# Two degree sums of A moved from the fifth strip of an attention to the first, and the last row block loaded at its 20 rows

## The chip, the cores and the metric

The kernel runs on one core of one Trainium2 chip. The metric is the device time of one execution in microseconds (us). The time before is the median of three runs, 733.3 us (730.9 to 733.57).

## The reference

The graph has 2708 nodes with 128 features and a dense 0/1 adjacency matrix A in float32. Layer 0 needs, among other things, the degree of each node (the row sums of A), and an attention over neighbours; layer 1 is left out here except for its last line, since the change does not touch it.

```python
deg = jnp.clip(adj.sum(axis=1), 1.0)
dis = deg ** (-0.5)
adj_norm = dis[:, None] * adj * dis[None, :]
diffusion = adj_norm @ x - x
norms = jnp.maximum(jnp.linalg.norm(x, axis=-1), COS_EPS)
sim = x @ x.T / (norms[:, None] * norms[None, :])
attn = jax.nn.softmax(beta * sim * adj, axis=1)
...
return diffusion + jax.nn.sigmoid(alpha) * (attn @ x - x)
...
x = _layernorm(x + _L0_gnn_ref(L0_gnn_t, x, adj, L0_gnn_alpha, L0_gnn_beta), axis=-1)
x = _layernorm(x + _L1_gnn_ref(x, adj, L1_gnn_W, L1_gnn_a), axis=-1)
```

## The kernel before

The nodes are cut into NB = 22 blocks of P = 128 (the last, block 21, has LAST = 20 valid nodes) and into NS = 6 strips of SW = 512 columns (the last has 148). A and its transpose are both in HBM; they are padded with zero rows to 22 full blocks.

**The attention** (lines 496 to 641) goes over the strips in the order 2, 3, 4, 0, 1, 5. The position in this order is n, from 0 to 5: "the first strip" is n = 0, "the fifth" is n = 4, and the narrow strip of 148 columns comes last, n = 5. Within a strip it goes over all 22 blocks, and k counts them from 0 to 21. For each k, TensorE makes the similarities `sim` in a PSUM bank (a matmul from the normalized rows `xn_t`, lines 560 to 563; or, where the same block pair has been computed in an earlier strip, four transposes of what was kept in `turned`, lines 553 to 558). VectorE multiplies them by `gentle` and by a piece of A (`piece`) into `p_t` (line 565), ScalarE takes the exponential in place (`grown`, line 591), GpSimd adds it to `total` (line 594), and TensorE accumulates `att_acc` from it (`weighed`, line 603). The buffers are four PSUM banks for `sim`, six for `p_t` and five for `piece`.

**The degrees** ride along in the attention. `degree(ib, h)` (line 456) loads one half row block of A, 128 x 1354 (677 KB), into one of two `row` buffers through SyncE's queue, and ScalarE copies it in place with a running sum into `deg2[:, ib, h]`. The 44 half rows stand in `todo` in the order of the blocks; the table `rows_at` (line 519) says at which k of which strip the next one is taken. `roots(b0, b1)` (line 465) turns the sums of a stretch of blocks into `dis`: three small operations on VectorE (writing `deg`, `live`, `deg`) and one power on GpSimd. It is called for blocks 0 to 7 at n = 2, for 8 to 17 at n = 4, k = 5, and for 18 to 21 at n = 4, k = 19 (line 514).

In the first strip two more things lie on ScalarE: the normalized rows are copied from PSUM to `xn_t` after they have been transposed (`turn_rows`, line 365). At k = 17 this is done for blocks 4 to 7, which are taken from k = 18 on (line 527).

**The last strip** (n = 5) also scales `x_sb` by `dis` in place (line 636), in five operations on VectorE over 6, 6, 5, 3 and 2 blocks. They have to wait until the attention's matmuls have read the rows they overwrite.

**The diffusion** follows (lines 776 to 782 and 865 on): for each strip, 22 matmuls with the scaled `x_sb` and a strip of the transpose (`strip`), which `load_strip` (line 765) loads in two halves of 11 blocks, 2.8 MB each, through SyncE's queue. Strips 0, 1 and 5 are loaded ahead of the diffusion. GpSimd issues loads of `nat`, 768 KB each, on its own queue (line 693); the first four stand right behind its last `total`.

**What sets the order.** Each engine runs its instructions in one order fixed when the program is built. A scheduler places them by priority and by a cost model; instructions made through `pinned` keep the order in which they were written on their engine. The whole first strip up to k = 20 is pinned on all engines (`strict`), `degree` pins its ScalarE copy everywhere, and `in_order` pins what it wraps. SyncE issues loads in its own order too, and waits there for the buffer of each.

Of the kernel before, what the change touches and what calls it, by code (L numbers as in the profile page):

```python
# [10 lines left out]
AF = mybir.ActivationFunctionType  # L11
# [4 lines left out]
P = 128  # L16
N = 2708
D = 128
NB = (N + P - 1) // P
# [26 lines left out]
def grouped(  # L46
# [14 lines left out]
    nc = tc.nc  # L61
# [10 lines left out]
    def width(s):  # L72
        return min(SW, N - s * SW)
# [86 lines left out]
    deg2 = const.tile([P, NB, 2], F32, name="deg2")  # L160
# [11 lines left out]
    def pinned(engine, op, *args, **kwargs):  # L172
        with ExitStack() as e:
            if engine in latest:
                e.enter_context(tc.issue_after(latest[engine].ins))
            latest[engine] = op(*args, **kwargs)  # L176
            return latest[engine]
# [31 lines left out]
    def to_sbuf(acc, v, nb):  # L209

        t = lp.tile([P, SW], F32, tag="to_rows", name="tr_sb", bufs=2)
        if v < nb * P:
            nc.gpsimd.memset(t[:, v : nb * P], 0.0)
        act("copy", t[:, :v], acc[:, :v])
        return t

    def turned(t, nb, ps):

        rows = ps.tile([P, SW // P, P], F32, tag="tp", name="tr_ps")
        for b in range(nb):  # L220
            mm(nc.tensor.transpose, rows[:, b, :], t[:, ts(b, P)], ident)
        return rows
# [76 lines left out]
    with ExitStack() as es:  # L299
# [156 lines left out]
        def degree(ib, h):  # L456

            z = pa.tile([P, N // 2], F32, tag="row", name="row", bufs=2)
            nc.sync.dma_start(z, adj[ts(ib, P), h * (N // 2) : (h + 1) * (N // 2)])
            pinned(  # L460
                "ACT", nc.scalar.activation, z, z, AF.Copy,
                accum_out=deg2[:, ib, h : h + 1],
            )

        def roots(b0, b1):
# [25 lines left out]


        todo = [(ib, h) for ib in range(NB) for h in range(2)]
        ended = None
        scaled = set()
        for n, s in enumerate(order):
# [4 lines left out]
            if v < nb * P:  # L501
# [15 lines left out]
            }  # L517

            rows_at = {
                0: (18, 20), 1: range(0, NB, 2), 2: range(0, NB, 2), 3: range(0, NB, 2),  # L520
                4: range(0, 18, 2), 5: (),
            }
            turns = {
                3: lambda: turn_rows(12, 16, by_dve),
# [20 lines left out]
            for k, jb in enumerate(blocks_j):  # L545
# [77 lines left out]
                if k in rows_at[n]:  # L623
                    in_order(lambda: degree(*todo.pop(0)))
# [73 lines left out]
    for q in range(4):  # L698
        i, end = KEPT * SW + q * quarters[1], KEPT * SW + (q + 1) * quarters[1]
        c = 0  # L700
        while i < end:
            s = min(i // SW, NS - 1)
            n = min(end, s * SW + width(s)) - i
# [80 lines left out]
    def mixed(s, rows):  # L784

        h = work2.tile([P, SW // P, D], F32, tag="h", name="h")
        for b in range(blocks(s)):
            ib = s * 4 + b
            dve(
                "scalar_tensor_tensor", h[:, b, :], rows[:, b, :], dis[:, ib : ib + 1],  # L790
                att[:, ib, :], ALU.mult, ALU.add,
            )
        return h
# [71 lines left out]
    for s in range(NS - 2):  # L865
# [7 lines left out]
        h = mixed(s, turned(to_sbuf(acc, v, nb), nb, ps_tp))  # L873
# [531 lines left out]
    for b0 in range(0, NB, 4):  # L1405
        n = min(4, NB - b0)
# [46 lines left out]
    for p0, p1 in PARTS:  # L1453
# [4 lines left out]
        for kb in range(0, NB, step) if p0 < TAIL else (0,):  # L1458
            n = min(step, NB - kb)
# [4 lines left out]
            else:  # L1464
                a, n = last, NB
# [7 lines left out]
        ib = p0 // P  # L1473
# [6 lines left out]
        for b0 in range(0, nb, 4):  # L1480
            n = min(4, nb - b0)
# [449 lines left out]
```

## Time and profile before

| Figure | Value |
|---|---|
| median of three runs | 733.3 us (730.9 to 733.57) |
| the profiled execution: its own time | 729.28 us |
| its span, first to last instruction | 727.5 us |
| mean granted TensorE clock | 0.989 |
| half rows on ScalarE: count, median of one | 44, 1.317 us |
| attention, about | 9 to 224 us of the span |
| of it the last strip, n = 5, about | 200 to 224 us |
| diffusion, about | 218 to 342 us |

The profiled execution took 1.8 us more than its span and was faster than the lowest of the three runs. In the profile, times are microseconds from the start of the span. PE is TensorE's matmuls, PEld its weight loads, DVE VectorE, ACT ScalarE, POOL GpSimd, SP SyncE. A bracket behind an instruction, such as [1.49 <-ACT p_t L195], says how long its engine sat idle before it and which work ended that. Matmul records come two for one float32 matmul and one for a transpose. PEclk is the clock granted to TensorE as a share of full speed. A matmul's end is modelled, so TensorE can be shown as busy while it runs at a lower rate; PEclk tells that.

### The profile page before, as it was taken

The page shows a single profiled execution, that of the slowest core. Times are in us where ns is not written, and L with a number is a line of the kernel's source. Part 1 is how long each engine was busy: PE and PEld are TensorE (multiplying, and loading weights), DVE is VectorE, ACT ScalarE, POOL GpSimd, SP SyncE. Part 2 cuts the span into 40 slices and gives each one's busy share as a digit, 9 for nine tenths or more (in the row PEclk, how much of TensorE's full clock was granted, in tenths as well). Part 3 has the DMA queues.
Part 4 walks back from the last instruction along what each step waited for, and adds up shares of the span by engine and source line. Part 5 has one row for each costly group of instructions (what it writes and reads, how often), then busy time and mean ns, then how long its engine had stood idle before and what let it go on. Part 6 is the DMA issues. An engine that isn't in the chain of part 4 may idle for free. (4 is left out here: it accounts for less than half of the span.)

```text
span 727.5 us, 7944 instructions
## 1 busy us (share of the span) xinstructions
PE 702.9 (97%) x2639; PEld 354.5 (49%) x2639; DVE 440.1 (61%) x921; ACT 421.0 (58%) x605; POOL 233.2 (32%) x240
## 2 busy tenths in 40 slices
PE   7999999999999999999988999999999999999995
PEld 4454444646474444446664444444444446444444
DVE  5676857666552433243996999999999884003032
ACT  4757877869751211121386999999999993000000
POOL 5868678878852000000005222222222200000000
PEclk9999999999979999999999999999999999999998
DMA  8868989999899999930868984444444631999970
GB/s 281 315 220 297 332 305 342 346 316 300 284 391 373 365 395 348 351 130 1 287 227 271 232 223 166 157 158 158 157 158 157 202 116 55 303 311 314 299 225 24
DMA packets 69778, 179.88 MB, mean 247 GB/s; under 512 B 6750, under 2 KB 20866, under 8 KB 66706
## 3 DMA queue, kind: packets, MB, share of 16 engines
q1 hardware_dynamic: 57188, 133.32, 53.4%
q0 software_dynamic: 6336, 43.08, 17.8%
q10 hardware_dynamic: 6206, 2.90, 1.4%
q8 instruction: 23, 0.38, 0.2%
q14 instruction: 25, 0.20, 0.1%
HBM read 176.44 MB, written 2.84 MB: 246 GB/s over the span
## 5 line engine op out<-in xcount | busy, mean ns | idle before, releaser
L201 POOL TENSOR_TENSOR total<-total,p_t 128x512 f32<-128x512 f32 (+3 forms) x111 | 124.6, 1124 | 38.7 <-ACT p_t L195 33.3
L176 PE MATMUL m_acc<-q,xws 128*128 128x512 f32 x240 | 121.2, 592 | 0.0
L190 DVE SCALAR_TENSOR_TENSOR p_t<-sim,gentle,piece 128x512 f32<-128x512 f32 (+1 forms) x111 | 72.1, 669 | 49.3 <-PE sim L185 39.6
L176 PE MATMUL num<-ring,wt 128*128 128x512 f32 x216 | 98.1, 546 | 2.9 <-DVE q L176 2.2
L185 PE MATMUL att_acc<-p_t,x_sb 128*128 128x512 f32 (+1 forms) x228 | 97.5, 554 | 2.7 <-ACT p_t L195 2.5
L185 PE MATMUL dif_acc<-strip,x_sb 128*128 128x512 f32 x220 | 97.7, 594 | 0.0
L195 ACT ACTIVATE p_t<-p_t,shift 128x512 f32<-128x512 f32 (+1 forms) x111 | 69.3, 655 | 35.8 <-DVE p_t L190 30.6
L176 DVE SCALAR_TENSOR_TENSOR q<-sr_b,nc_s,q 128x1536 f32<-128x1536 f32 (+1 forms) x48 | 77.8, 1623 | 16.6 <-ACT q L176 16.5
L176 DVE COPY q<-num 128x512 f32<-128x512 f32 (+1 forms) x142 | 83.4, 611 | 3.7 <-PE num L176 3.7
L176 PEld LDWEIGHTS m_acc<-q,xws 128*128 128x128 f32 x240 | 45.4, 190 | 56.0 <-issue 55.7
L1468 PE MATMUL h_acc<-ring,m_sb 128*128 128x512 f32 x164 | 72.3, 593 | 0.0
L176 ACT ACTIVATE q<-q,head,rest 128x1536 f32<-128x1536 f32 (+1 forms) x48 | 70.2, 1508 | 1.5 <-DVE ring L176 1.2
L176 ACT ACT_TABLE_LOAD x52 | 66.7, 1283 | 3.8 <-issue 2.9
L185 PEld LDWEIGHTS dif_acc<-strip,x_sb 128*128 128x128 f32 x220 | 40.7, 190 | 47.8 <-issue 47.8
L176 ACT ACTIVATE q<-q,c_s 128x1536 f32<-128x1536 f32 (+1 forms) x48 | 62.9, 1355 | 0.3
L185 PEld LDWEIGHTS att_acc<-p_t,x_sb 128*128 128x128 f32 x228 | 40.7, 201 | 45.8 <-ACT p_t L195 25.6
L176 ACT ACTIVATE row<-row 128x1354 f32<-128x1354 f32 x44 | 58.1, 1321 | 7.8 <-DMA row<-in_adj 7.7
L176 PEld LDWEIGHTS num<-ring,wt 128*128 128x128 f32 x216 | 39.0, 190 | 48.3 <-issue 34.2
L1478 ACT COPY ht<-h_acc 128x512 f32<-128x512 f32 (+1 forms) x6 | 3.2, 536 | 91.3 <-PE h_acc L1468 91.2
L1483 DVE TENSOR_TENSOR hh<-rows,x 128x512 f32<-128x512 f32 (+1 forms) x6 | 3.8, 641 | 84.1 <-PE rows L1402 81.7
L176 POOL DMA_INDIRECT ring<-in_adj_t,k_no x18 | 21.0, 1169 | 97.7 <-PE num L176 92.7
L1468 PEld LDWEIGHTS h_acc<-ring,m_sb 128*128 128x128 f32 x164 | 30.8, 190 | 36.8 <-issue 36.8
(286 smaller groups left out, 897.2 us busy)
## 6 DMA issues: line engine op xcount, KB each, us to landing
row<-in_adj SPq DMA_DIRECT2D x44, 677.0 KB, 4.9
strip<-in_adj_t SPq DMA_DIRECT2D x10, 2816.0 KB, 16.8
piece<-in_adj_t SPq DMA_DIRECT2D x24, 1024.0 KB, 6.9
ring<-in_adj_t SPq DMA_DIRECT2D x20, 1024.0 KB, 5.0
nat<-in_adj_t SPq DMA_DIRECT2D x13, 768.0 KB, 6.0
x_sb<-in_adj_t SPq DMA_DIRECT2D x7, 1024.0 KB, 5.1
nat<-in_adj_t POOLq DMA_DIRECT2D x9, 768.0 KB, 10.1
piece<-in_adj_t SPq DMA_DIRECT2D x7, 512.0 KB, 5.8
```

The costliest lines, as they stand in the source:

```text
L176: latest[engine] = op(*args, **kwargs)
L185: op(*args, **kwargs)
L190: return getattr(nc.vector, op)(*args, **kwargs)
L195: return getattr(nc.scalar, op)(*args, **kwargs)
L201: getattr(nc.gpsimd, op)(*args, **kwargs)
L1468: nc.tensor.matmul(acc[:, : h1 - h0], m_sb[:, kb + b, :], a[:, b, h0:h1], start=(kb + b == 0), stop=(kb + b == NB - 1),)
L1478: nc.scalar.copy(ht[:, h0:h1], acc[:, : h1 - h0])
L1483: nc.vector.tensor_tensor(hh[:, b0 : b0 + n, :], rows[:, :n, :], x1[:, ib + b0 : ib + b0 + n, :], ALU.add)
```

## The change

`rows_at` gives the first strip two more half rows, at k = 14 and 16, and the fifth strip two fewer, at k = 14 and 16. Since `todo` is taken in order, every half row from the first on is taken two places earlier. `degree` loads and sums only the valid rows of a block, which is 20 rather than 128 rows for block 21 and the same as before for all others. Since the 108 other entries of `deg2` for block 21 are no longer written by `degree`, GpSimd clears the block's two columns once at the start.

```diff
         def degree(ib, h):
 
             z = pa.tile([P, N // 2], F32, tag="row", name="row", bufs=2)
-            nc.sync.dma_start(z, adj[ts(ib, P), h * (N // 2) : (h + 1) * (N // 2)])
+            n = min(P, N - ib * P)
+            nc.sync.dma_start(
+                z[:n], adj[ib * P : ib * P + n, h * (N // 2) : (h + 1) * (N // 2)]
+            )
             pinned(
-                "ACT", nc.scalar.activation, z, z, AF.Copy,
-                accum_out=deg2[:, ib, h : h + 1],
+                "ACT", nc.scalar.activation, z[:n], z[:n], AF.Copy,
+                accum_out=deg2[:n, ib, h : h + 1],
             )
...
         todo = [(ib, h) for ib in range(NB) for h in range(2)]
+        nc.gpsimd.memset(deg2[:, NB - 1, :], 0.0)
...
             rows_at = {
-                0: (18, 20), 1: range(0, NB, 2), 2: range(0, NB, 2), 3: range(0, NB, 2),
-                4: range(0, 18, 2), 5: (),
+                0: (14, 16, 18, 20), 1: range(0, NB, 2), 2: range(0, NB, 2), 3: range(0, NB, 2),
+                4: range(0, 14, 2), 5: (),
             }
```

The order of instructions of the changed program, which the build gives, differs from before in these places. On ScalarE the two new half rows stand in the first strip behind the exponentials of k = 14 and 16, the second of them ahead of the copy to `xn_t` of k = 17; the last two half rows, which stood behind the exponential of k = 19 of the last strip, are gone from there, and the two before them have 20 rows. On VectorE the three operations of `roots(18, NB)` move from the end of the last strip to between `p_t` of k = 9 and the first scaling of `x_sb`, and the scaling of blocks 14 to 19 moves from behind them to between `p_t` of k = 14 and 15. On GpSimd the power of `roots(18, NB)` and two clearings (`e2_w`, `x1`) move from the end of the last strip to behind the `total` of k = 5 and 6. On TensorE two diffusion matmuls rather than seven stand ahead of the last two `att_acc` of the last strip. On SyncE's queue the last two half rows, 677 KB each, no longer stand between the two halves of strip 0.

## The prediction, made before the changed kernel ran

> **What bounds the kernel now.** I read the page's busy shares first, then stretches of the attention, then the timelines of the two places where the change puts and removes work.
>
> ```profile
> PE 702.9 (97%) x2639; PEld 354.5 (49%) x2639; DVE 440.1 (61%) x921; ACT 421.0 (58%) x605; POOL 233.2 (32%) x240
> ```
>
> TensorE is busy 97% of the span, so an edit on another engine pays only where TensorE waits for it. In the first strip TensorE runs back to back but for one wait, for ScalarE's copy into `xn_t` at k = 13. The change puts a half row ahead of the next such copy. Here is TensorE's timeline, then ScalarE's:
>
> ```profile
> 35.35 1.12 PE L176 MATMUL sim<-xn_t 128*128 128x512 f32 x2 [0.76 <-ACT xn_t L176]
> ...
> 42.77 1.02 PE L176 MATMUL sim<-xn_t 128*128 128x512 f32 x2
> ```
> ```profile
> 37.36 0.72 ACT L176 ACTIVATE p_t<-p_t,shift 128x512 f32<-128x512 f32 x1 [1.44 <-DVE p_t L176]
> ...
> 40.81 0.72 ACT L176 ACTIVATE p_t<-p_t,shift 128x512 f32<-128x512 f32 x1 [0.99 <-DVE p_t L176]
> 41.44 0.56 ACT L176 COPY xn_t<-xn_ps 128x512 f32<-128x512 f32 x1
> ...
> 45.29 1.32 ACT L176 ACTIVATE row<-row 128x1354 f32<-128x1354 f32 x1
> ...
> 46.61 0.71 ACT L176 ACTIVATE p_t<-p_t,shift 128x512 f32<-128x512 f32 x1
> ```
>
> The exponentials of k = 14 and 16 (and the one between) have 1 us or more of air before them. The copy of k = 17 has none behind it: it ends at 42.00, and the matmul of 42.77 (k = 18) needs it. At the other end, from the full timeline of the end of the attention:
>
> ```profile
> 195.35 1.33 ACT L176 ACTIVATE row<-row 128x1354 f32<-128x1354 f32 x1 [0.71 <-DMA row<-in_adj]
> ...
> 197.44 1.12 PE L185 MATMUL att_acc<-p_t,x_sb 128*128 128x512 f32 x2 [1.49 <-ACT p_t L195]
> ...
> 200.33 1.33 ACT L176 ACTIVATE row<-row 128x1354 f32<-128x1354 f32 x1 [1.40 <-DMA row<-in_adj]
> ...
> 217.58 1.32 ACT L176 ACTIVATE row<-row 128x1354 f32<-128x1354 f32 x1
> ...
> 217.73 0.52 PE L185 MATMUL att_acc<-p_t,x_sb 128*128 128x148 f32 x2 [0.28 <-ACT p_t L195]
> ...
> 218.08 6.17 PE L185 MATMUL dif_acc<-strip,x_sb 128*128 128x512 f32 x14
> ...
> 222.28 0.96 DVE L636 TENSOR_TENSOR x_sb<-x_sb,dis 128x768 f32<-128x768 f32 x1 [1.37 <-POOL dis L176]
> ```
>
> The last two half rows (217.58 and the next, up to 220.2) delay `dis` and a scaling to 222.28, but TensorE has seven diffusion matmuls from 218.08 on and doesn't idle. The half rows that do hold it up stand at 195.35 and before. Last, the clock in stretches of 3.41 us:
>
> ```profile
> core 0: us, PE busy (x) PEld busy (x) DVE busy (x) ACT busy (x) POOL busy (x), PEclk, DMA share, GB/s
> 199.35:202.76 3.41, 3.41 (x23) 2.68 (x21) 1.78 (x6) 2.43 (x5) 2.74 (x5) 1.00 1.04 376
> 202.76:206.17 3.41, 3.41 (x13) 2.43 (x12) 1.56 (x5) 2.85 (x8) 2.21 (x6) 0.50 1.05 396
> 206.17:209.59 3.42, 3.42 (x13) 2.28 (x14) 1.33 (x2) 0.63 (x2) 1.40 (x3) 0.50 1.06 401
> 209.59:213.00 3.41, 3.41 (x16) 3.00 (x15) 2.24 (x8) 1.34 (x4) 0.70 (x2) 0.50 1.02 397
> 213.00:216.40 3.40, 3.40 (x23) 2.69 (x22) 1.77 (x5) 1.58 (x5) 2.79 (x6) 1.00 1.05 388
> ```
>
> TensorE has half its clock for 10.24 us in the last strip. That is the largest loss near the change: 10.24 x 0.5 = 5.1 us if all of it is TensorE's own work.
>
> **The change part by part.**
>
> Half rows at k = 14 and 16 of the first strip. One costs ScalarE 1.32 us to the next instruction (45.29 to 46.61). The first starts at 37.36 + 0.62 = 37.98 (0.62 is the spacing 44.67 to 45.29 of exponential and half row) and ends at 39.30: the exponential of k = 15 comes 0.21 us late, and `att_acc` runs three blocks behind, so nothing waits. The second starts at 41.43 and moves the copy from 41.44 to 42.75, its end to 43.31, and the matmul of k = 18, with the 0.05 us of 35.30 to 35.35, to 43.36 rather than 42.77: **+0.59 us**. The matmuls behind it can't pass, since the strip's order is pinned. Their loads are the two half rows that SyncE issues at 16.15, long landed. Those of k = 18 and 20 are then issued as the buffers free, at about 39.5 and 43, ahead of one piece that isn't issued before 43 in any case; at 4.9 us to landing (median of half rows) they are there at 44.4 and 47.9, for slots at 45.9 and 49.3. Bounds: 0.4 to 1.5 us, the upper if the second slips. Later strips have their half rows in the same slots, so their waits for loads (0.5 to 1.1 us) remain, and so does the idle 1.49 us.
>
> Half rows of 20 rows. No row shows ScalarE on 20 partitions; GpSimd's `total` takes 0.50 us at 128x148 and 0.75 us at 20x148, so fewer rows save nothing there. By the Trainium skill, "ScalarE: Activation LUTs" (What ACT_TABLE_LOAD costs) an activation costs per element of the free dimension, all lanes at once, and the free size stays 1354. I take 1.32 us as before, not 20/128 of it. By the other reading 2 x 1.1 us would go, in a place where TensorE works off `sim` transposes anyway; both give 0. What shrinks is the load, and so the wait of 1.40 us at 200.33. The exponential behind it then waits for VectorE (about 201.0) rather than 201.66. But its `att_acc` stands on TensorE behind transposes until 203.66, so I take 0; bounds 0 to -0.66.
>
> Two half rows less at 217.58. ScalarE gets 2.63 us back, under the cover of the diffusion: 0. With the exponentials 1 or 2 blocks earlier the 0.28 us wait goes: **-0.3 us**.
>
> Work moved into the last strip's middle. VectorE: three operations of 0.16 to 0.17 us fall into its idle 1.71 us before the first scaling. The scaling of 0.96 us between k = 14 and 15 must wait for the `att_acc` of k = 11 (213.12 + 0.42 = 213.54), so `p_t` of k = 15 comes at about 214.5 rather than 213.13. Its exponential ends at 215.3, and TensorE, with the new order, reaches that `att_acc` at about 215.5 (0.93 us for each pair of transposes and two `att_acc` from 212.38 on). Value 0, bounds 0 to +1.2. GpSimd: 1.02 + 0.68 + 0.19 us; `total` of k = 6 is done at about 209.2, and `p_t` of k = 12 reuses its buffer at 211.5: 0. The early clearing of 128x2 lies in GpSimd's wait for VectorE (4.0 us longest): 0.
>
> The DMA queue. SyncE moves 2 x 0.68 MB later in the old order, and 2 x 0.57 MB are not moved at all; 2.5 MB less between 195 and 213, about 6.4 us at 390 GB/s. No matmul of the diffusion waits for a strip, so this gives 0. One thing comes sooner: GpSimd's four `nat` loads, issued at 223.68, wait only for its last `total`, at about 220.2 with the change. Their effect is a rival below.
>
> Sum: 0.59 - 0.3 = +0.3 us: the profiled execution of 729.28 would be 729.6. The three runs have their median 4 us higher; the difference applies to it: 733.6 us.
>
> **The rivals.**
>
> Faster: the half clock is a result of ScalarE's waits and goes with them. The Trainium skill, "TensorE: Matmul & The Clock Gate" (Part 1, The HAM clock gate, and Part 4, PE-mode transpose), says that the clock falls after a window of about 3.4 us with little activity, and that transposes don't count. The row alone says that TensorE was busy 3.41 of 3.41 us in the window ahead of the fall. By the row nothing was wrong but the waits around it, and removing them could give back up to 5.1 us: 728.5. By the rule the window 199.35 to 202.76 is the cause: it holds 0.95 us of `att_acc` (up to 200.3), then only transposes and sums. The changed order has the same transposes there, so the half clock stays. The 10.24 us, three times 3.41, speak for the rule. I follow it; but the windows run free of the kernel, so a fall can be one window longer or shorter (1.7 us) in any run.
>
> Slower: the scaling put between k = 14 and 15. If the `att_acc` of k = 15 waits for it by over 0.2 us, TensorE idles up to 1.2 us just where the clock should recover, and the half clock lasts one window more: 0.6 + 1.2 + 1.7 = 3.5 us, 736.8. Against it stands the recovery at 213.0, before that point.
>
> Slightly slower: the earlier `nat`. While it moves, SyncE's queue is left with little:
>
> ```profile
> q0 software_dynamic: 537, 3.00, 73.4%
> q1 hardware_dynamic: 546, 1.09, 29.5%
> ```
>
> (10 us from 228, packets, MB and share.) Strip 1's first half, issued at 219.43 behind the last `p_t`, landed at 230.7 by its packets; TensorE needs it at 238.1. With `nat` from 224 rather than 227.6, both together (2.88 + 3.15 MB at 0.40 MB/us from 220.6) are done at 235.7: the margin falls from 7.4 to about 2 us. Beyond that each us is paid in full; I give it 1 us, 734.6.
>
> **How the numbers follow.** No change to speak of (733.6, its bounds 732 to 735.5): 0.6. Faster by a shorter or missing half clock (728.5 to 732): 0.18. Slower by the scaling (735.5 to 737.5): 0.14. Earlier `nat` (734.6): 0.08. The range 730.0 to 736.8 leaves out the ends of the two outer cases. About 0.5% (3.7 us) is what a measurement of this kernel can tell from no change. Faster by more: 0.14; slower by more: 0.13; within: 0.73.
>
> **What would show it.** The `sim` matmul of k = 18 in the first strip with a new wait of about 0.6 us for ScalarE's `xn_t`; an idle of about 1.5 us before the fifth strip's late `att_acc` still there; no half rows behind k = 5 of the last strip, the 20-row ones at 1.32 us; the half clock again for about 10 us; strip 1 without a wait. Wrong would be: a clock that doesn't fall, an `att_acc` of k = 15 that waits, or a `dif_acc` that waits for a DMA.

## The result and the profile after

The changed kernel takes 732.75 us (median of 20 runs, 730.53 to 738.42), beside 730.68 us (728.22 to 733.57) of the kernel before in 20 runs on the same chip. The ratio is 1.0033, with a 95% interval of 1.0020 to 1.0047: slower by 0.33%, or 2.4 us (1.5 to 3.4). The three runs that the prediction started from had a median 2.6 us above that of these twenty, so it is the difference that is to be compared: +0.3 us forecast, +2.4 us measured, and both lie within the 0.5% that the prediction called no change to speak of. That 732.75 us stands so near the 733.6 us forecast is luck: the start was 2.6 us too high, and the change cost 2.1 us more than forecast. Measured once more (the last experiment) the ratio was 1.0016 (0.9998 to 1.0035). The two intervals overlap between 1.0020 and 1.0035.

The profiled execution took 731.85 us, its span is 730.1 us (727.5 before). From the page after:

```profile
PE 703.7 (96%) x2639; PEld 354.3 (49%) x2639; DVE 440.6 (60%) x921; ACT 420.6 (58%) x605; POOL 235.0 (32%) x241
```

The work of the engines is that of before, within 0.8 us on TensorE, ScalarE and VectorE. TensorE's idle time grew from 24.6 to 26.4 us, so most of the loss lies in idle stretches. The first is in the first strip, on TensorE's timeline and then on ScalarE's:

```profile
41.67 1.02 PE L176 MATMUL att_acc<-p_t,x_sb 128*128 128x512 f32 x2
43.13 1.12 PE L176 MATMUL sim<-xn_t 128*128 128x512 f32 x2 [0.44 <-ACT xn_t L176]
```
```profile
40.57 0.72 ACT L176 ACTIVATE p_t<-p_t,shift 128x512 f32<-128x512 f32 x1 [0.80 <-DVE p_t L176]
41.20 1.32 ACT L176 ACTIVATE row<-row 128x1354 f32<-128x1354 f32 x1
...
42.51 0.56 ACT L176 COPY xn_t<-xn_ps 128x512 f32<-128x512 f32 x1
42.98 0.72 ACT L176 ACTIVATE p_t<-p_t,shift 128x512 f32<-128x512 f32 x1
```

The half row of k = 16 (41.20) stands ahead of the copy, the copy ends at 43.07, and `sim` of k = 18 starts behind it. The other half row, of k = 14, leaves no bracket on TensorE in the first strip.

The second place is the fifth strip. TensorE's waits from 172 to 202 us of the changed kernel, and ScalarE's half rows there:

```profile
182.41 1.13 PE L185 MATMUL att_acc<-p_t,x_sb 128*128 128x512 f32 x2 [0.22 <-ACT p_t L195]
193.67 2.84 PE L185 MATMUL att_acc<-p_t,x_sb 128*128 128x512 f32 x6 [1.74 <-ACT p_t L195]
200.11 1.12 PE L185 MATMUL att_acc<-p_t,x_sb 128*128 128x512 f32 x2 [0.74 <-ACT p_t L195]
```
```profile
187.70 1.33 ACT L176 ACTIVATE row<-row 128x1354 f32<-128x1354 f32 x1 [0.25 <-DMA row<-in_adj]
191.59 1.33 ACT L176 ACTIVATE row<-row 128x1354 f32<-128x1354 f32 x1 [2.46 <-DMA row<-in_adj]
196.22 1.33 ACT L176 ACTIVATE row<-row 128x1354 f32<-128x1354 f32 x1 [1.38 <-DMA row<-in_adj]
198.02 1.33 ACT L176 ACTIVATE row<-row 128x1354 f32<-128x1354 f32 x1 [0.37 <-DMA row<-in_adj]
201.50 1.31 ACT L176 ACTIVATE row<-row 20x1354 f32<-20x1354 f32 x1
204.37 1.32 ACT L176 ACTIVATE row<-row 20x1354 f32<-20x1354 f32 x1
```

Before there was one wait of 1.49 us; now there are three, 2.70 us in sum. ScalarE stands at 191.59 for 2.46 us behind a half row whose load has not landed, with the exponentials queued behind it. The two half rows with 20 rows take as long as those with 128.

The end of the attention, from the full timeline, went as forecast: no half row is left there, the last `att_acc` has no bracket, and two diffusion matmuls (four records) stand ahead of it.

```profile
218.94 1.98 PE L185 MATMUL dif_acc<-strip,x_sb 128*128 128x512 f32 x4
...
220.76 0.67 PE L185 MATMUL att_acc<-p_t,x_sb 128*128 128x148 f32 x4
221.26 3.17 PE L185 MATMUL dif_acc<-strip,x_sb 128*128 128x512 f32 x7
...
221.46 0.55 DVE L640 TENSOR_TENSOR x_sb<-x_sb,dis 128x256 f32<-128x256 f32 x1 [1.25 <-PE att_acc L185]
```

And the half clock came back in the last strip (the columns are those of the prediction's table):

```profile
199.35:202.76 3.41, 2.67 (x12) 1.62 (x11) 1.56 (x5) 3.41 (x8) 2.48 (x2) 1.00 0.59 153
202.76:206.17 3.41, 3.41 (x22) 2.50 (x21) 2.55 (x8) 2.68 (x8) 2.62 (x7) 1.00 1.03 398
206.17:209.59 3.42, 3.42 (x15) 2.39 (x15) 1.45 (x7) 2.15 (x6) 1.49 (x3) 0.61 1.05 391
209.59:213.00 3.41, 3.41 (x15) 2.84 (x14) 2.11 (x6) 0.00 (x0) 3.25 (x7) 0.50 1.06 380
213.00:216.40 3.40, 3.40 (x21) 2.68 (x19) 2.59 (x8) 1.35 (x4) 2.77 (x6) 0.89 1.05 387
```

It lasts 6.83 us here (206.94 to 213.76), two stretches of 3.41 us rather than three. At half speed one such stretch is worth up to 1.7 us, so this execution has that much luck in it, and the loss in its span (2.6 us) is smaller than the waits alone would make it. Where the two traces part, by the start of the same matmul in each: -0.2 us ahead of k = 14 of the first strip, +0.7 us over the rest of that strip, +0.6 us in the next three, +1.6 us in the fifth, -1.7 us in the last and up to 240 us (the shorter half clock above all), and +1.7 us between 366 and 393 us, in layer 1, where no instruction of the change lies.

### The profile page after: what moved, and what is told of

Read it like the earlier page. It is cut to its first block, busy times and chain, and to the rows that moved or that the text cites. A ratio compares the mean times of both kernels' runs of the same rounds, so it can differ in the third digit from the quotient of the medians.

```text
span 730.1 us, 7946 instructions
## 1 busy us (share of the span) xinstructions
PE 703.7 (96%) x2639; PEld 354.3 (49%) x2639; DVE 440.6 (60%) x921; ACT 420.6 (58%) x605; POOL 235.0 (32%) x241
## 5 line engine op out<-in xcount | busy, mean ns | idle before, releaser
L176 ACT ACTIVATE row<-row 128x1354 f32<-128x1354 f32 (+1 forms) x44 | 58.2, 1323 | 13.2 <-DMA row<-in_adj 13.2
```

## The experiments

Theory A is the prediction's own sum: the move pays at `sim` of k = 18 in the first strip. The rival, B, is that the 20-row loads, or the work that comes early into the last strip, cost the time. Later theories are named where they come up.

All were timed in five rounds beside the kernel before on the same chip, and each left one profiled execution. Since single executions differ by the half clock and by when loads land, a wait in one trace is taken as caused by an edit only where it stands in every trace with that edit and in none without.

**The kernel before, unchanged**, for the spread.

> The kernel before, unchanged, as a control and for a second trace. All theories: ratio 1.000 within 0.15%. If the slowdown of the change is a chance pattern of load waits in single executions, this trace too should show half-row waits on ScalarE well away from 7.7 us (8 waits); if the waits belong to the kernel, they should be within 1.5 us of 7.7.

Measured: 0.9998 (0.9985 to 1.0011). Its fifth strip has one wait of 1.76 us (1.49 in the first trace), its half clock lasts 6.83 us. So these two vary by themselves. ScalarE's half rows wait 8.3 us for loads, within the 1.5 us of 7.7 that was to mean that the waits belong to the kernel.

**One half of the change at a time.** First the two half rows moved, with all loads at 128 rows and no clearing:

```diff
-                0: (18, 20), 1: range(0, NB, 2), ...
-                4: range(0, 18, 2), 5: (),
+                0: (14, 16, 18, 20), 1: range(0, NB, 2), ...
+                4: range(0, 14, 2), 5: (),
```

> Only the move: two half rows at k = 14 and 16 of the first strip, none at k = 14 and 16 of the fifth; the last block is loaded with 128 rows. Theory A (the copy to xn_t behind the half row of k = 16 costs about 0.5 us and the rest is later load waits that come with the shift of the half rows): +2 us, a wait of 0.4 to 0.6 us at the sim matmul of k = 18, half-row waits on ScalarE of 11 to 15 us in all. Rival B (the 20-row loads and the early work on VectorE and GpSimd in the last strip cost the time): +0.3 us.

Measured: 1.0022 (1.0004 to 1.0040). The half rows wait 7.6 us for loads, not the 11 to 15 of theory A, and yet TensorE's three waits of the fifth strip are there, 2.73 us in sum. Then the loads of 20 rows with the clearing, and the half rows where they were:

> Only the 20-row loads: half rows in their old places, the last block loaded and summed at 20 rows. Theory A: 0 us (-0.5 to +0.3), half-row waits near 7.7 us. Rival B: +1.5 to +2 us.

Measured: 1.0000 (0.9983 to 1.0016). The move carries the loss; what the 20-row loads cost or bring is too small to be seen. In the first of the two the wait of 0.44 us at k = 18 is there again, in the second it isn't.

**The half row out of the copy's way**, k = 15 in the place of 16:

```diff
-                0: (14, 16, 18, 20), 1: range(0, NB, 2), ...
+                0: (14, 15, 18, 20), 1: range(0, NB, 2), ...
```

> The changed kernel with the second new half row at k = 15 rather than 16, so that the copy to xn_t of k = 17 starts about 0.4 us late instead of 1.3 and ends before TensorE needs it. Theory A: the wait at the sim matmul of k = 18 is gone and the time is 0.5 us lower than the changed kernel (about +1.5 us on before); theory A1 (that wait is all of the slowdown, through what it shifts later): +0 us. Rival B: +2 us, as the changed kernel.

Measured: 1.0035 (1.0019 to 1.0052). The wait at k = 18 is gone, and nothing is won. Its trace shows what came in its place in the second strip, on ScalarE, then on TensorE:

```profile
54.00 1.32 ACT L176 ACTIVATE row<-row 128x1354 f32<-128x1354 f32 x1
58.37 1.33 ACT L176 ACTIVATE row<-row 128x1354 f32<-128x1354 f32 x1 [1.74 <-DMA row<-in_adj]
```
```profile
60.46 1.98 PE L185 MATMUL att_acc<-p_t,x_sb 128*128 128x512 f32 x4 [1.20 <-ACT p_t L195]
```

The half row behind the one at 54.00 waits for its load, and the exponential behind it makes TensorE wait 1.20 us. The median time from issue to landing of the half rows between 36 and 64 us is 7.3 us here and 5.1 us in the changed kernel, at nearly the same bytes (7.76 and 7.99 MB). Why the loads landed later was not found.

**The two strips apart.** From here on theory R says that the fifth strip's price comes from `roots(8, 18)`: with the half rows taken earlier, its three VectorE operations stand five `p_t` earlier in the strip, so ScalarE's pairs of half rows come closer together in time. The list of moved instructions ahead of the prediction leaves this move out, and so does the prediction's sum. First the first strip alone: the kernel before, with half rows 0 and 1 taken twice.

```diff
-        todo = [(ib, h) for ib in range(NB) for h in range(2)]
+        todo = [(0, 0), (0, 1)] + [(ib, h) for ib in range(NB) for h in range(2)]
...
-                0: (18, 20), 1: range(0, NB, 2), ...
+                0: (14, 16, 18, 20), 1: range(0, NB, 2), ...
```

> The kernel before, with two more half rows at k = 14 and 16 of the first strip; the first two half rows are simply taken twice, so every later strip keeps its half rows, its roots and its SyncE order as before (46 half rows, 1.4 MB more read). Theory F (the first strip alone pays, as the prediction's sum has it): ratio about 1.001 (+0.6 us, the sim of k = 18 waits 0.44 us), fifth strip with one att_acc wait of 1.5 to 1.8 us as before. Theory F+ (the first strip starts a shift of loads that costs later, whatever the fifth strip's order is): 1.003. Theory R (roots(8, 18) earlier in the fifth strip costs 1.2 us): 1.001, the rest is missing here.

Measured: 1.0025 (1.0009 to 1.0042), which holds the 1.001 of theory F and the 1.003 of F+. The wait at k = 18 is there (0.44 us), the fifth strip's is 1.47 us as before. Beyond these, a load came late once in the second strip, and cost TensorE 1.56 us at 86.06.

Then everything but the first strip: the changed kernel without the half rows of block 0.

```diff
-        todo = [(ib, h) for ib in range(NB) for h in range(2)]
+        todo = [(ib, h) for ib in range(1, NB) for h in range(2)]
         nc.gpsimd.memset(deg2[:, NB - 1, :], 0.0)
+        nc.gpsimd.memset(deg2[:, 0, :], 1.0)
...
-                0: (14, 16, 18, 20), 1: range(0, NB, 2), ...
+                0: (18, 20), 1: range(0, NB, 2), ...
```

> The changed kernel without the half rows of block 0 (their sums are set to 1, so the degree of block 0 is left out of the computation); the first strip keeps its two half rows at k = 18 and 20, everything from the second strip on is in the changed kernel's order. Theory F+: 1.000 or below. Theory R: about 1.0015 (+1.2 us in the fifth strip, less the 0.28 us wait at the end of the attention), att_acc waits of 2.5 us in sum in the fifth strip. If both this and the first-strip kernel come out at 1.000, the cause lies in the two together.

Measured: 1.0010 (0.9993 to 1.0026), which holds what either theory expected. Its trace is against theory R: the fifth strip has the changed kernel's order of half rows, exponentials and `roots`, and waits less than before.

```profile
184.65 3.70 PE L185 MATMUL att_acc<-p_t,x_sb 128*128 128x512 f32 x8 [0.54 <-ACT p_t L195]
196.92 1.12 PE L185 MATMUL att_acc<-p_t,x_sb 128*128 128x512 f32 x2 [0.34 <-ACT p_t L195]
```

**The roots late again**, in the changed kernel:

```diff
-                (4, 5): lambda: roots(8, 18),
+                (4, 14): lambda: roots(8, 18),
```

> The changed kernel with roots(8, 18) called at k = 14 rather than 5 of the fifth strip, which brings its three VectorE operations back to behind eight p_t and its GpSimd power back to behind fourteen total, as in the kernel before; all other engines' orders are those of the changed kernel. Theory R: the fifth strip's att_acc waits fall from 2.7 us to 1.5 us, ratio about 1.0015 (from 1.0033). Theory F+ or load timing by chance: 1.0033, no change against the changed kernel.

Measured: 1.0035 (1.0015 to 1.0055). The waits in the fifth strip did what theory R says, the time did not:

```profile
197.66 1.82 PE L185 MATMUL att_acc<-p_t,x_sb 128*128 128x512 f32 x2 [1.54 <-ACT p_t L195]
```

One wait of 1.54 us, as before, but no gain that the timing can see. This kernel's mean clock in its runs is 0.987, though, that of before in the same series 0.991. And with both remedies:

```diff
-                (4, 5): lambda: roots(8, 18),
+                (4, 14): lambda: roots(8, 18),
...
-                0: (14, 16, 18, 20), 1: range(0, NB, 2), ...
+                0: (14, 15, 18, 20), 1: range(0, NB, 2), ...
```

> The same, and the first strip's half rows at k = 14, 15, 18, 20, so that the sim of k = 18 doesn't wait. Theory R with the prediction's first-strip term: 1.000 to 1.001 (no slower than before). If only the fifth strip matters: 1.0015. If neither matters: 1.0033.

Measured: 1.0055 (1.0037 to 1.0073), the slowest of all, where 1.000 to 1.001 was expected. The late half row behind 54 us is there again (1.47 us on ScalarE at 58.09, 0.92 us on TensorE), and half rows take 7.4 us to landing between 36 and 64 us, so both traces with the half row at k = 15 have it. It isn't that slot's alone: a half row waits 1.92 us at the same place in a later trace with one at k = 16. The fifth strip has waits of 0.89 and 1.67 us, though the roots stand as before. So the place of `roots` alone doesn't decide what the fifth strip waits.

The two times don't decide against theory R. If all the slow clock were TensorE's own work, it would cost a run its span times (1 - mean clock). By this estimate, an upper one, the two kernels with late roots lose 2.6 and 3.6 us more to the clock than before does, which is nearly their whole loss of 2.6 and 3.7 us (differences of means). The three with two rows moved and early roots (the move alone, k = 15, the changed kernel measured again) lose 1.6 to 2.4 us at clocks no lower than before's. Late roots may have removed one loss and brought another; no run separates the two.

Two theories were left. Theory W: the wait at k = 18 is the first strip's whole price, and the rest is chance of single executions. Theory L: each further half row in the first strip makes later loads late.

**One half row at a time**, in the kernel before with half row 0 taken twice; first at k = 14, then at k = 16:

```diff
-        todo = [(ib, h) for ib in range(NB) for h in range(2)]
+        todo = [(0, 0)] + [(ib, h) for ib in range(NB) for h in range(2)]
...
-                0: (18, 20), 1: range(0, NB, 2), ...
+                0: (14, 18, 20), 1: range(0, NB, 2), ...
```

> The kernel before with one more half row, at k = 14 of the first strip (half row 0 is taken twice, so all later strips keep theirs). No half row stands ahead of the xn_t copy, so sim of k = 18 should not wait. Theory W (the wait at k = 18 is what the first strip costs, and all above it is chance of the single executions): 1.000. Theory L (a further half row in the first strip, with its load, makes later loads and so later half rows late, with or without that wait): 1.001 or more, with one more att_acc wait of 0.9 to 1.7 us somewhere in strips two to five, as the profiled executions with two more rows show in five of six.

> The same with the one more half row at k = 16, ahead of the xn_t copy. Theory W: the wait of 0.44 us at sim of k = 18 is back, +0.7 us, ratio 1.001, and above the kernel with the row at k = 14. Theory L: about the same as with the row at k = 14, 1.001 to 1.002, or their sum of 0.7 us more.

Measured: 1.0005 (0.9984 to 1.0026) with k = 14, 1.0018 (1.0001 to 1.0034) with k = 16. The two differ by one line of ScalarE's order, and their traces start within 0.03 us of each other. TensorE at k = 18 with the half row at k = 14, then with it at k = 16:

```profile
41.49 1.02 PE L176 MATMUL att_acc<-p_t,x_sb 128*128 128x512 f32 x2
42.35 1.02 PE L176 MATMUL sim<-xn_t 128*128 128x512 f32 x2
43.21 1.02 PE L176 MATMUL att_acc<-p_t,x_sb 128*128 128x512 f32 x2
```
```profile
41.47 1.02 PE L176 MATMUL att_acc<-p_t,x_sb 128*128 128x512 f32 x2
42.93 1.13 PE L176 MATMUL sim<-xn_t 128*128 128x512 f32 x2 [0.44 <-ACT xn_t L176]
43.89 0.59 PE L176 MATMUL att_acc<-p_t,x_sb 128*128 128x512 f32 x1
```

Without the wait each matmul starts 0.16 us before the shown end of the one ahead (41.49 + 1.02 = 42.51, start 42.35). With it `sim` starts 0.58 us later (0.60 from the earlier `att_acc`) and takes 0.11 us longer, so the next `att_acc` is 0.68 us late (0.70): a bracket of 0.44 us costs 0.70 us. The times don't contradict this: 0.0013 of 730 us is 0.9 us, but the uncertainty of that difference, from the two intervals, is about 2 us. The half row at k = 14 costs nothing that can be measured, as theory W says; but both traces show a late load in strips two to five (0.81 us on TensorE at 91.75, 1.38 us at 61.23), so theory L isn't excluded.

**Half of the move**, in the changed kernel:

```diff
-                0: (14, 16, 18, 20), 1: range(0, NB, 2), ...
-                4: range(0, 14, 2), 5: (),
+                0: (14, 18, 20), 1: range(0, NB, 2), ...
+                4: range(0, 16, 2), 5: (),
```

> The changed kernel with only one half row moved: first strip k = 14, 18, 20, fifth strip without k = 16 alone; 20-row loads as in the changed kernel; one 20-row half row stays at the end of the last strip. Theory W: no wait at k = 18, ratio 1.000. Theory L: 1.001 or more.

Measured: 0.9980 (0.9965 to 0.9994), median 727.31 us: faster than the kernel before (729.31 us in the same series) and than the changed kernel (730.87 us there). This is the version to keep, though neither theory foresaw a gain. Its profiled execution, 725.84 us, is the fastest of its 22 runs. Its waits of TensorE, then of ScalarE for half rows, between 30 and 224 us (sum, times, longest):

```profile
PE att_acc L185 <- ACT p_t L195: 1.4, 4, 0.7
PE sim L176 <- ACT xn_t L176: 0.8, 1, 0.8
```
```profile
ACT row L176 <- DMA row<-in_adj: 4.8, 7, 1.3
```

The same rows of the kernel before:

```profile
PE att_acc L185 <- ACT p_t L195: 2.5, 4, 1.5
PE sim L176 <- ACT xn_t L176: 0.8, 1, 0.8
```
```profile
ACT row L176 <- DMA row<-in_adj: 7.7, 8, 1.4
```

And of the changed kernel:

```profile
PE att_acc L185 <- ACT p_t L195: 3.8, 6, 1.7
PE sim L176 <- ACT xn_t L176: 1.2, 2, 0.8
```
```profile
ACT row L176 <- DMA row<-in_adj: 13.2, 14, 2.5
```

The 4.8 us are the least of all traces, but this sum doesn't follow the time: with two half rows moved it lies between 6.6 and 13.2 us, with half rows as before between 7.7 and 8.3. The gain in time is measured, its cause is open. By the estimate above, at most 0.8 us of it are the clock (0.991 in the mean, before 0.990).

**The changed kernel, unchanged.**

> The changed kernel once more, unchanged, for a second profiled execution and a second interval: ratio 1.0033 within 0.0015; the wait of 0.44 us at k = 18 in the trace again. If the fifth strip's waits of 1.74 and 0.74 us are fixed by the order they are there again; if they are chance of one execution they differ.

Measured: 1.0016 (0.9998 to 1.0035), just below the range expected. The wait of 0.44 us at k = 18 is there; the 0.28 us at the end are gone here too. The fifth strip has 0.22, 1.52 and 0.40 us, at the same three places as in the first trace (182, 193 and 199 us); the trace of the move alone has all three, that of k = 15 the first two, and no other kernel waits at the second, the longest. So these waits repeat with two rows moved and early roots, and aren't chance of one execution.

The waits of the fifth strip in all executions (us, summed, ahead of `att_acc` from 172 to 202 us):

| Half rows moved, fifth strip's order | Waits |
|---|---|
| none or first strip only, order of before (six traces) | 1.49, 1.76, 1.66, 1.47, 1.93, 1.77 |
| two moved, roots early (four traces) | 2.70, 2.14, 2.73, 1.51 |
| two moved, roots late (two traces) | 1.54, 2.56 |
| roots early, first strip as before (one trace) | 0.88 |
| one moved (one trace) | 0.83 |

What the rows with early roots differ in can be seen on VectorE. The first operation of `roots(8, 18)` in the changed kernel, then in the kernel with the first strip as before:

```profile
177.16 1.09 DVE L176 TENSOR_TENSOR deg<-deg 128x10 f32<-128x10 f32 x1
```
```profile
176.43 0.16 DVE L176 TENSOR_TENSOR deg<-deg 128x10 f32<-128x10 f32 x1
```

It takes 0.97 to 1.09 us in the four traces of the second row (one of which, with 1.51 us, waits no longer than before), and delays the `p_t`, the exponentials and so the half rows behind it. In these it ends 0.05 us before an addition to `total` starts on GpSimd (178.25 and 178.30 in the first); in the kernel that waits 0.88 us it begins while GpSimd is idle. With late roots it takes 0.35 us where the waits are 1.54 us, and 0.90 where they are 2.56; in the order of before, 0.32 to 0.35 us. It isn't all: with one moved it takes 0.86 us, but there VectorE is idle for 2.10 us ahead of it, and the waits are 0.83 us. This is read from the traces; no run tested it.

## Why the prediction was right, and where it was not

**Half rows at k = 14 and 16.** Right in place and nearly in size. k = 14 is free, k = 16 moves the copy and `sim` of k = 18. `sim` was forecast 0.59 us late and was 0.60 us late. What the sum left out is that the matmul behind a wait takes 0.11 us longer, so the term is 0.70. The wait stands in all six traces with a half row at k = 16 and in none of the eight without.

**Half rows of 20 rows.** Right: 1.31 and 1.32 us beside 1.317, and a kernel with this edit alone at 1.0000. The prediction chose what the Trainium skill says ("ScalarE: Activation LUTs", What ACT_TABLE_LOAD costs: the cost goes by elements of the free dimension) over 20/128 of the time, and the trace agrees.

**Two half rows less at the end.** Right: the last `att_acc` has no wait in the seven traces without half rows there, and one of 0.28 us (0.45 once) in the seven with them.

**Work moved into the last strip's middle, and the queue.** Right as far as the diffusion goes: no `att_acc` waits for the scaling, no `dif_acc` for a load. Once, with half rows at k = 14 and 15 and late roots, a `dif_acc` waited 0.24 us for the scaling. For layer 1, see the end of this section.

**The half clock.** Right: it is there in all fourteen executions, for 6.83 or 10.24 us in the last strip and in some for 3.41 us elsewhere, always whole stretches of 3.41 us but for the one at the very end of the program, as the rule says that the prediction followed (the Trainium skill, "TensorE: Matmul & The Clock Gate", Part 1, The HAM clock gate). How many of them there are differs from run to run of one kernel: among the changed kernel's twenty runs the four at a clock of 0.992 have a median of 731.83 us, the three at 0.984 one of 737.0 us. It isn't only chance, since the mean clock of 22 runs differs between kernels (0.986 with both remedies, 0.991 before in the same series); what in a kernel sets it was not found.

**The step that failed** is this one: "Later strips have their half rows in the same slots, so their waits for loads (0.5 to 1.1 us) remain, and so does the idle 1.49 us." The slots are the same, the waits are not: half rows on ScalarE waited 13.2 us for loads in one trace of the changed kernel and 9.3 in the other (7.7 before), and TensorE's 1.49 us in the fifth strip became 2.70 and 2.14. The sum of ScalarE's waits isn't what counts (7.6 us with the move alone, and TensorE still waits 2.73 us), but which load is late: the half row at 191.59 waited 2.46 us. The prediction treated these waits as a constant and gave this no bound; even in the kernel before they reach 1.29 us in the fifth strip, not 1.1. It also left out that `roots(8, 18)` moves in that strip.

The sum with what was measured: +0.70 for k = 16, -0.28 for the end, +0.4 to +1.2 in the fifth strip (2.14 to 2.70 less 1.49 to 1.76, rounded) make +0.8 to +1.6 us, where the two measurements say +2.4 and +1.2. What stays open: what sets the waits in the fifth strip. The place of `roots` alone doesn't, the first strip alone doesn't raise them, the rest alone lowers them; the length of the operation shown above is the best clue. Taking the half rows' loads out, or giving them a third buffer, would tell more; neither was run.

The stretch from 366 to 393 us, in layer 1, is open too, but it has a pattern. Against the first trace of before, six of the seven kernel traces without half rows at the end of the attention lose 1.4 to 2.9 us there (1.7 in both of the changed kernel; k = 15 only 0.2). All others lie between -0.2 and +0.2 us, but for one at +1.0. In three of the six a half clock of 3.41 us falls there. So part of the price seems to come from what the change moves at the end of the attention, the prediction's rivals of the scaling and the earlier `nat` among it, and it shows only in layer 1; no run separates them. With 1.7 us for it the sum would be +2.5 to +3.3 us.

## What to carry to other kernels

A unit of work on an engine with idle time is free only if nothing that the bottleneck waits for is queued behind it: two places in the order, k = 14 and 16, both have about 1 us or more of idle time ahead and differ by 0.7 us, because the copy stands behind one of them. Where loads run with two buffers, as here, their waits can move with a shift of their consumers, so forecast such a wait as a range and try neighbouring placements: one half row moved is 0.2% faster than before, two are 0.2 to 0.3% slower. And where one execution differs from the next by 1.7 us for each slow clock stretch, a difference of 2 us needs some twenty runs of each kernel (here they gave 1 to 1.5 us either way), the mean clock of these runs belongs beside their times, and a trace shows the place of a loss only where the wait repeats.

## What was not expected of the hardware

A bracket understates its price: 0.44 us of idle time cost TensorE 0.70 us, since the overlap of 0.16 us with the matmul ahead is lost and the matmul behind takes 1.13 us for 1.02. The same 7.8 to 8.0 MB between 36 and 64 us came at a median of 5.1 us to landing for a half row in the changed kernel (both traces) and at 7.3 and 7.4 us in the two with the half row at k = 15 in the place of 16. And a VectorE operation on 128 x 10 values took between 0.16 and 1.09 us, ending with GpSimd's addition where it was long.
